# One tile of some groups read from on-chip features instead of gathered from DRAM, in a graph layer on one core

## The chip, the core and the metric

The kernel runs on one core of a Trainium2 chip. The engines of that core are TensorE (PE in the profile, with its weight loads as PEld), VectorE (DVE), ScalarE (ACT), GpSimd (POOL) and SyncE (SP). The metric is the device time of one execution in microseconds; the time given for a kernel is the median of several executions.

## The reference, cut to what matters

There are 12500 nodes with 64 features and 212500 edges with 32 features each, sorted by their destination `col`. Everything is float32.

```python
msg_in = concat([nodes[row], nodes[col], edge_features])       # 64 + 64 + 32 columns
messages = relu(msg_in @ mW1 + mb1) @ mW2 + mb2
aggregated = segment_sum(messages, col, num_segments=12500)
upd = relu(concat([nodes, aggregated]) @ uW1 + ub1) @ uW2 + ub2
out = layernorm(nodes + upd)
```

Two facts of the algebra matter. `nodes[col] @ mW1[64:128]` has only as many different rows as there are different destinations. And `mW2` may be applied after the sum, so that only `relu(...)` and a count per node have to be summed per edge.

## The kernel before

**Groups and tiles.** Edges are taken in groups of 384, three tiles of 128, and there are 554 groups (`G`), the last one not full. As edges are sorted by destination, a group touches at most 32 neighbouring destinations (`W`), its window.

**What one group needs.** `gather(g)` issues one indirect DMA for each of the three tiles: 128 rows of 64 features of `x`, one for each edge's source, from DRAM into `own.s[g % 20]`, by GpSimd (line L132). `onehot(g)` writes beside them, on VectorE (L306), a 128 x 32 one-hot block that tells the edge's place in the window. `turn(g)` transposes each tile of 96 columns on TensorE (L318), and ScalarE copies the result, 96 x 384, into `own.st` and sums the one-hots on the way into `own.counts` (L326). `hidden(g)` multiplies it with a weight tile `own.wm` of 128 rows on TensorE (L339); the 128 rows are 32 rows of the window's own products (made by `windows`, L292, and copied by VectorE, L297), 64 rows of `mW1` for the source's features and 32 rows for the edge's, which SyncE loads beside the transposed tile (L266). ScalarE applies the relu (L349). `sums(g)` multiplies with the one-hots on TensorE (L365), and VectorE adds the result to `agg` and the counts to a row of `xc` (L374, L375) at an address taken from a register.

**Node features on the chip.** `xc` holds all node features transposed, 64 partitions by 12500 columns, with a row of counts in front and a row of ones behind. `places` reads from it with a register address (L285) what `windows` needs, after a load of four registers (L278); that is done once for four groups.

**Order.** The order on every engine is that of the program text; nothing reorders it. Step k runs `turn(k)`, `hidden(k - 2)` and `sums(k - 4)` as one block on TensorE, and then ScalarE's and VectorE's follow-up work. Only the last matmul of a step signals. The blocks alternate between two PSUM sets (`own.ps`), so a step may start only when the follow-up of the step two before is done. Before each step VectorE makes the one-hots of the next one; after it GpSimd gets `gather(k + 16)`.

**Rings.** `own.s` has 20 slots, so the gathers of a group wait for ScalarE's copy of the group 20 before (`copy_by[g - RING]`); `own.h` has 3 slots, `own.st` 3 blocks of four groups, `own.wm` 8. In the last 10 groups the parts are separate steps, and no gather is left to issue. Chunks of 512 finished nodes are updated, normalised and stored in between (`step_update`).

Of the kernel before, what the change touches and what calls it, by code (L numbers as in the profile page):

```python
# [12 lines left out]
I32 = mybir.dt.int32  # L13
AF = mybir.ActivationFunctionType
ALU = mybir.AluOpType
ET = mybir.EngineType
# [3 lines left out]
P = 128  # L20
N = 12500
E = 212500
D = 64
# [5 lines left out]
W = 32  # L29
TG = 3  # L30
GE = TG * P
G = (E + GE - 1) // GE
SB = 4
# [9 lines left out]
BITS = 16  # L43
NEAR_GROUPS = 24
SHORT = 10
TIMES = 4


def tiles_of(g):

    n = min(GE, E - g * GE)
    return [min(P, n - j * P) for j in range((n + P - 1) // P)]
# [23 lines left out]
class Own:  # L76
# [4 lines left out]
    def __init__(self, nc, ctx):  # L81
        def on(name, *shape, of=nc.sbuf_tensor):
            return ctx.enter_context(of(name, list(shape), F32)).ap()

        self.s = [on(f"own_s{i}", P, TG, W + D) for i in range(RING)]
        self.st = [on(f"own_st{i}", P, SB * GE) for i in range(BLOCKS)]
        self.wm = [on(f"own_wm{i}", P, H) for i in range(NW)]
        self.h = [on(f"own_h{i}", P, TG, H) for i in range(NH)]
        self.ident = on("own_ident", P, P)
        self.counts = on("own_counts", D + W, G)  # L90

        self.ps = [on(f"own_ps{i}", P, 3, 512, of=nc.psum_tensor) for i in range(2)]
# [3 lines left out]
def ordered(ctx: ExitStack, tc: tile.TileContext, a, own, ok):  # L96
# [10 lines left out]
    temp = early.enter_context(tc.tile_pool(name="temp", bufs=1))  # L107
    ident, wm, counts = own.ident, own.wm, own.counts


    src_sb = const.tile([P, NT], I32, name="src_sb")
    first = AHEAD * TG
    nc.sync.dma_start(src_sb[:, :first], a["src"][:, :first])

    loads, places_by, copy_by, relu_by, sums_by, wm_by, turn_by = ({} for _ in range(7))
    efs_by, hidden_by = {}, {}

    def after(first, *others):

        tc.declare_no_dep(first.ins, group="quiet", reason="waits for the last of a step")  # L120
        for i in others:
            tc.add_manual_dep(
                first.ins, i.ins.name,
                mybir.DependencyInfo(mybir.DependencyClass.Sync, mybir.DependencyReason.DATA),
                reason="the kernel's own rings",
            )
        return first

    def gather(g):
        s = own.s[g % RING]  # L130
        loads[g] = [
            nc.gpsimd.indirect_dma_start(  # L132
                out=s[:p, j, W:], out_offset=None, in_=x[:, :],
                in_offset=bass.IndirectOffsetOnAxis(
                    ap=src_sb[:p, g * TG + j : g * TG + j + 1], axis=0),
            )
            for j, p in enumerate(tiles_of(g))
        ]
        for i in loads[g]:
            after(i, *([copy_by[g - RING]] if g >= RING else []))  # L140
# [7 lines left out]
    for g in range(AHEAD):  # L148
# [6 lines left out]
    zero = const.tile([P, NP // P], F32, name="zero")  # L155
    nc.vector.memset(zero, 0.0)
    nc.vector.tensor_copy(ident, ident_t)
    iota = iop.tile([P, W], F32, name="iota")
    nc.vector.tensor_copy(iota, iota_i)

# [4 lines left out]
    nc.sync.dma_start(first_i, a["firsts"].to_broadcast([P, G]))  # L165
    dlc_i = temp.tile([P, G * TG], I32, name="dlc_i")
    nc.sync.dma_start(dlc_i, a["dst_cols"])
    nc.sync.dma_start(xc[0:1, :].rearrange("o (p n) -> o p n", p=P), zero)
    nc.sync.dma_start(xc[D + 1 :, :].rearrange("o (p n) -> o p n", p=P), ones[:, : NP // P])
    w1b = const.tile([D + 2, H], F32, name="w1b")  # L170
    nc.vector.memset(w1b[0:1, :], 0.0)
    nc.scalar.dma_start(w1b[1 : D + 1, :], a["mW1"][D : 2 * D, :])
    nc.scalar.dma_start(w1b[D + 1 :, :], a["mb1"][None, :])
    nc.scalar.dma_start(xc[1 : D + 1, :NEAR_NODES], a["xT"][:, :NEAR_NODES])

    wm_loads = [
        [nc.sync.dma_start(t[W : W + D, :], a["mW1"][:D, :]),
         nc.sync.dma_start(t[D + W :, :], a["mW1"][2 * D :, :])] for t in wm
    ]

    def bit(k):

        nodes = [NEAR_NODES + (N - NEAR_NODES) * i // BITS for i in (k, k + 1)]
        tiles = [first + (NT - first) * i // BITS for i in (k, k + 1)]
        nc.sync.dma_start(src_sb[:, slice(*tiles)], a["src"][:, slice(*tiles)])
        nc.sync.dma_start(xc[1 : D + 1, slice(*nodes)], a["xT"][:, slice(*nodes)])


    first_f = own.ps[0].rearrange("p a b -> p (a b)")[:, :G]
# [22 lines left out]
    u1s = const.tile([D, H], F32, name="u1s")  # L212
    nc.scalar.dma_start(u1s, a["uW1"][D:, :])
    ux = const.tile([D + 1, H], F32, name="ux")
    nc.scalar.dma_start(ux[1 : D + 1, :], a["uW1"][:D, :])
# [11 lines left out]
    nc.vector.tensor_copy(ux[0:1, :], wps[0:1, 1])  # L227

# [59 lines left out]
    def windows(b, wp, own_bank=True):  # L288


        xw, n = xws.pop(b)
        did = nc.tensor.matmul(wp[: n * W, :], xw[:, :n, :], w1b, start=True, stop=True)  # L292

        def copies():
            for i in range(n):
                g = b * SB + i
                c = nc.vector.tensor_copy(wm[g % NW][:W, :], wp[i * W : (i + 1) * W, :])  # L297
                after(c, *([did] if own_bank else []), *([hidden_by[g - NW]] if g >= NW else []))
                wm_by[g] = c

        return did, copies

    def onehot(g):
        if g >= G:
            return
        places_by[g] = nc.vector.tensor_tensor(  # L306
            own.s[g % RING][:, :, :W], iota.unsqueeze(1).to_broadcast([P, TG, W]),
            dlc[:, g * TG : (g + 1) * TG].unsqueeze(2).to_broadcast([P, TG, W]), ALU.is_equal,
        )
        after(places_by[g], *([sums_by[g - RING]] if g >= RING else []))  # L310

    def turn(g, ps):


        s = own.s[g % RING]
        xt = ps[: D + W, 0, :GE]
        did = [
            nc.tensor.transpose(xt[:, j * P : j * P + p], s[:p, j, :], ident[:p, :p])  # L318
            for j, p in enumerate(tiles_of(g))
        ]  # L320

        def copy(step):
            t, c, n = columns(g)
            turn_by[g] = step
            copy_by[g] = after(
                nc.scalar.activation(t[: D + W, c : c + n], xt[:, :n], AF.Copy,  # L326
                                     accum_out=counts[:, g : g + 1]), step)
            if g >= BLOCKS * SB:
                after(copy_by[g], hidden_by[g - BLOCKS * SB])
            return [copy_by[g]]  # L330

        return did, [*loads.pop(g), places_by[g]], copy

    def hidden(g, ps):
        t, c, n = columns(g)
        sizes = tiles_of(g)
        pre = ps[:, 1, : TG * H].rearrange("p (j h) -> p j h", h=H)
        did = [
            nc.tensor.matmul(pre[:p, j, :], t[:, c + j * P : c + j * P + p], wm[g % NW],  # L339
                             start=True, stop=True)  # L340
            for j, p in enumerate(sizes)
        ]
        needs = [copy_by[g], wm_by[g], efs_by[g // SB], *(wm_loads[g] if g < NW else ())]
# [12 lines left out]

        return did, needs, relu

    def sums(g, ps):
        h, s = own.h[g % NH], own.s[g % RING]  # L360
        sizes = tiles_of(g)
        sg = ps[:, 2, : (TIMES + 1) * W].rearrange("p (t w) -> p t w", w=W)
        did = [nc.tensor.transpose(sg[0:1, TIMES, :], counts[:W, g : g + 1], ident[:W, :W])]  # L363
        for j, p in enumerate(sizes):
            did.append(nc.tensor.matmul(  # L365
                sg[:, :TIMES, :], h[:p, j, :],
                s[:p, j, :W].unsqueeze(1).to_broadcast([p, TIMES, W]),
                start=j == 0, stop=j == len(sizes) - 1))

        def add(step):  # L370
            sums_by[g] = step
            at = bass.ds(starts.pop(g), W)
            return [
                after(nc.vector.tensor_tensor(agg[:, at], sg[:, 0, :], agg[:, at], ALU.add), step),  # L374
                after(nc.vector.tensor_tensor(xc[0:1, at], sg[0:1, TIMES, :], xc[0:1, at],  # L375
                                              ALU.add), step),
            ]

        return did, [*relu_by[g], copy_by[g]], add
# [99 lines left out]
    for k in range(G):  # L479
# [21 lines left out]
                    made += 1  # L501
        if k + AHEAD < G:
            gather(k + AHEAD)
    while summed < G:
        step((sums, summed))
        summed += 1
# [329 lines left out]
```

## Time and profile before

| | |
|---|---|
| median of 10 runs | 2601.94 us (2600.3 to 2604.2) |
| the profiled execution | 2602.16 us, of which the span is 2600.4 us |
| PE, PEld busy | 1633.2 us (63%), 1425.7 us (55%) |
| POOL busy | 1569.7 us (60%) |
| DVE, ACT busy | 571.9 us (22%), 537.8 us (21%) |
| granted TensorE clock | 0.785 of full speed |
| gathers (L132) | 1661, 945 ns each |
| mean DMA rate | 37 GB/s |

No engine is busy for the whole span, so the shares alone do not name a bound. In the profile, an engine's idle time is put down to what ended it last; "issue" means that no wait is seen, and "remote" that the releaser is not known. Start and length of GpSimd's instructions are rough. The ends of matmuls are modelled.

### The profile page before, as it was taken

What the parts mean: (1) busy time and instruction counts of PE and PEld (TensorE: products, weight loads), DVE (VectorE), ACT (ScalarE), POOL (GpSimd) and SP (SyncE); (2) the same over time, 40 slices, a digit from 0 to 9 for tenths busy, and PEclk for the clock granted to TensorE, in tenths of its full rate; (3) what the DMA queues carried; (4) which work ended last, traced back from release to release, by engine and by line L of the source; (5) the groups of instructions that cost most, each with busy time, mean ns of one, the idle gap of its engine ahead of it and who ended that gap; (6) DMA issues with size and microseconds to landing.
All of it is one profiled execution on the core that took longest, in us unless ns stands there. A gap on an engine that the chain in (4) does not pass through costs nothing.

```text
span 2600.4 us, 30668 instructions
## 1 busy us (share of the span) xinstructions
PE 1633.2 (63%) x9441; PEld 1425.7 (55%) x9441; DVE 571.9 (22%) x3191; ACT 537.8 (21%) x1715; POOL 1569.7 (60%) x1668
## 2 busy tenths in 40 slices
PE   1356666666666666766666666756566666666677
PEld 0355555555555555655555555655555555655565
DVE  4012122221222221212212212212122122221222
ACT  0122122212222221212221222122122222222222
POOL 7566665666666666666666666666666666666650
PEclk9678777787787787778787877777787778777878
DMA  3211111111111111111111111111111111111110
GB/s 89 51 41 39 34 36 35 34 36 36 36 35 37 34 39 31 39 34 36 39 33 37 35 34 38 36 32 38 36 33 38 31 39 33 37 38 34 36 35 13
DMA packets 73364, 96.05 MB, mean 37 GB/s; under 512 B 33451, under 2 KB 40842, under 8 KB 73194
## 3 DMA queue, kind: packets, MB, share of 16 engines
q0 software_dynamic: 53152, 54.51, 12.0%
q1 hardware_dynamic: 19128, 39.03, 5.4%
q8 instruction: 80, 1.31, 0.2%
q14 instruction: 90, 0.74, 0.1%
q10 hardware_dynamic: 914, 0.46, 0.1%
HBM read 90.58 MB, written 3.20 MB: 36 GB/s over the span
## 4 chain that ended last, share of the span: by engine, by line
another core or an unknown queue 41%; PE 29%; issue 16%; ACT 11%; DVE 2%; DMA 0%; DVEq 0%; ACTq 0%
PE own_ps L365 10%; PE own_ps L339 8%; ACT own_h L349 5%; PE own_ps L318 5%; ACT own_st L326 5%; PE u_ps L405 2%; PE own_ps L363 1%; PE u_ps L392 1%; PE u_ps L393 1%; PE own_ps L292 1%; DVE own_wm L297 1%; ACT u L395 0%; DVE xc L375 0%; DMA u1s<-in_uW 0%
## 5 line engine op out<-in xcount | busy, mean ns | idle before, releaser
L132 POOL DMA_INDIRECT own_s<-in_x,src_sb x1661 | 1568.9, 945 | 956.6 <-issue 494.0
L318 PE MATMUL own_ps<-own_ident,own_s 128*96 128x128 f32 x1661 | 366.6, 343 | 832.1 <-ACT own_st L326 426.0
L318 PEld LDWEIGHTS own_ps<-own_ident,own_s 128*96 128x96 f32 x1661 | 234.0, 160 | 897.1 <-ACT own_st L326 443.6
L326 ACT ACTIVATE own_st<-own_ps 96x384 f32<-96x384 f32 x554 | 268.3, 484 | 1896.7 <-remote 1121.1
L365 PE MATMUL own_ps<-own_s,own_h 128*128 128x128 f32 x3322 | 633.1, 337 | 3.5 <-issue 3.5
L339 PE MATMUL own_ps<-own_wm,own_st 128*128 128x128 f32 x3322 | 612.9, 336 | 1.2 <-DVE own_wm L297 1.2
L339 PEld LDWEIGHTS own_ps<-own_wm,own_st 128*128 128x128 f32 x3322 | 570.9, 253 | 4.9 <-DVE own_wm L297 1.6
L365 PEld LDWEIGHTS own_ps<-own_s,own_h 128*128 128x128 f32 x3322 | 513.4, 231 | 29.4 <-issue 2.5
L374 DVE TENSOR_TENSOR agg<-own_ps,agg 128x32 f32 x554 | 106.1, 191 | 1870.4 <-ACT own_h L349 1352.1
L349 ACT ACTIVATE own_h<-own_ps 128x384 f32<-128x384 f32 x553 | 264.2, 478 | 17.2 <-PE own_ps L339 13.2
L297 DVE COPY own_wm<-own_ps 32x128 f32<-32x128 f32 x550 | 155.0, 282 | 7.0 <-issue 1.0
L306 DVE TENSOR_TENSOR own_s<-iota,dlc 128x96 f32<-128x96 f32 x554 | 132.9, 240 | 4.1
L363 PE MATMUL own_ps<-own_ident,own_counts 32*1 32x32 f32 x554 | 106.6, 192 | 4.0 <-ACT own_st L326 1.9
L326 ACT ACTIVATION_READ_ACCUMULATOR own_st<-own_ps 96x1 f32 x554 | 107.2, 194 | 0.0
L375 DVE TENSOR_TENSOR xc<-own_ps,xc 1x32 f32 x554 | 99.0, 179 | 19.8 <-PE u_ps L393 11.5
L363 PEld LDWEIGHTS own_ps<-own_ident,own_counts 32*1 32x1 f32 x554 | 41.1, 74 | 93.5 <-issue 46.3
L405 PE MATMUL u_ps<-u,u 128*128 128x64 f32 (+1 forms) x196 | 49.6, 404 | 29.9 <-ACT u L395 29.9
L405 PEld LDWEIGHTS u_ps<-u,u 128*128 128x128 f32 (+1 forms) x196 | 47.1, 324 | 32.5 <-ACT u L395 32.3
L392 PE MATMUL u_ps<-agg,wc 128*128 128x512 f32 (+1 forms) x50 | 35.5, 800 | 45.7 <-DVE agg L374 36.1
L285 DVE COPY xw<-xc 66x32 f32 x554 | 60.3, 170 | 2.9 <-DMA xc<-in_xT 2.3
L292 PE MATMUL own_ps<-w1b,xw 66*128 66x128 f32 (+1 forms) x276 | 59.0, 298 | 0.0
L292 PEld LDWEIGHTS own_ps<-w1b,xw 66*128 66x128 f32 (+1 forms) x276 | 48.0, 217 | 0.1
(58 smaller groups left out, 203.0 us busy)
## 6 DMA issues: line engine op xcount, KB each, us to landing
own_s<-in_x,src_sb POOLq DMA_INDIRECT x1661
own_st<-in_efT SPq DMA_DIRECT2D x138, 192.0 KB
xin<-in_x SPq DMA_DIRECT2D x24, 128.0 KB
out<-o SPq DMA_DIRECT2D x24, 128.0 KB
xc<-in_xT SPq DMA_DIRECT2D x12, 179.2 KB
dlc_i<-in_dst_cols SPq DMA_DIRECT2D x1, 831.0 KB
xc<-in_xT SPq DMA_DIRECT2D x4, 179.5 KB
src_sb<-in_src SPq DMA_DIRECT2D x13, 50.5 KB
```

Of the source, the lines that this page charges most:

```text
L132: nc.gpsimd.indirect_dma_start(out=s[:p, j, W:], out_offset=None, in_=x[:, :], in_offset=bass.IndirectOffsetOnAxis(ap=src_sb[:p, g * TG + ...
L292: did = nc.tensor.matmul(wp[: n * W, :], xw[:, :n, :], w1b, start=True, stop=True)
L297: c = nc.vector.tensor_copy(wm[g % NW][:W, :], wp[i * W : (i + 1) * W, :])
L306: places_by[g] = nc.vector.tensor_tensor(own.s[g % RING][:, :, :W], iota.unsqueeze(1).to_broadcast([P, TG, W]), dlc[:, g * TG : (g + 1) * ...
L318: nc.tensor.transpose(xt[:, j * P : j * P + p], s[:p, j, :], ident[:p, :p])
L326: nc.scalar.activation(t[: D + W, c : c + n], xt[:, :n], AF.Copy, accum_out=counts[:, g : g + 1]), step)
L339: nc.tensor.matmul(pre[:p, j, :], t[:, c + j * P : c + j * P + p], wm[g % NW], start=True, stop=True)
L349: relu_by[g] = [nc.scalar.activation(h, pre, AF.Relu)]
L363: did = [nc.tensor.transpose(sg[0:1, TIMES, :], counts[:W, g : g + 1], ident[:W, :W])]
L365: did.append(nc.tensor.matmul(sg[:, :TIMES, :], h[:p, j, :], s[:p, j, :W].unsqueeze(1).to_broadcast([p, TIMES, W]), start=j == 0, stop=j = ...
L374: after(nc.vector.tensor_tensor(agg[:, at], sg[:, 0, :], agg[:, at], ALU.add), step),
L405: nc.tensor.matmul(o_ps[:p, k], u[:, k:q:n], u2, start=True, stop=True)
```

## The change

From group 44 on, the last tile of every 16th group (31 tiles) and, from group 48 on, that of every 24th (21 tiles) is no longer gathered. Its 128 source columns are copied from `xc`, one instruction for each edge with a column address from a register, into a 128 x 128 tile `own.f` whose lower 64 rows are zero: by VectorE for the first kind, by ScalarE for the second. The copies of a tile are spread over the 16 or 24 steps that end 4 steps before the group's own, 8 a step on VectorE, 5 or 6 on ScalarE, behind the follow-up work of the step; eight registers are loaded ahead of each eight copies. For such a group, ScalarE's copy of the transposed tiles is made in two instructions (features of two tiles, one-hots of three), and TensorE multiplies the third tile in two matmuls, one for the copied columns and one for window and edge rows.

So that a copied column and the weight rows meet at the same partitions, features come first in every layout: in `own.s`, `own.wm`, `xc` and `w1b`. The counts are transposed from partitions 64 to 95 of `own.counts`. Four tiles of 128 columns are zeroed at the start, and one more small DMA loads the copied tiles' source numbers (`cols_sb`, 52 x 128).

```diff
+ONE = TG - 1
+BY_DVE = range(44, G - 16, 16)
+BY_ACT = range(48, G - 16, 24)
+COPIED = {**dict.fromkeys(BY_DVE, (ET.DVE, BY_DVE)), **dict.fromkeys(BY_ACT, (ET.Activation, BY_ACT))}
+SLACK = 3
+REGS = 8
...
-        self.s = [on(f"own_s{i}", P, TG, W + D) for i in range(RING)]
+        self.s = [on(f"own_s{i}", P, TG, D + W) for i in range(RING)]
...
-            for j, p in enumerate(tiles_of(g))
+            for j, p in enumerate(tiles_of(g)) if not copied(g, j)
...
+    for t in [t for pair in own.f.values() for t in pair]:
+        nc.vector.memset(t[D:, :], 0.0)
...
+    cols_sb = const.tile([len(COPIED), P], I32, name="cols_sb")
+    nc.sync.dma_start(cols_sb, a["src_rows"])
...
+    def source_columns(g):
+        _, way = COPIED[g]
+        return own.f[way][way.index(g) % 2]
+
+    def copies_of(k):
+
+        for n, (g, (engine, way)) in enumerate(COPIED.items()):
+            at = k - (g - SLACK - way.step)
+            if not 0 <= at < way.step:
+                continue
+            f, used, ahead = source_columns(g), g - 2 * way.step, held[engine]
+            for r in range(at * P // way.step, (at + 1) * P // way.step):
+                if r % REGS == 0:
+                    _, ahead[:] = nc.values_load_multi_w_load_instructions(
+                        cols_sb[n : n + 1, r : r + REGS], engines=[engine], min_val=0,
+                        max_val=N - 1,
...
+                    )
+                column = f[:D, r : r + 1], xc[:D, bass.ds(ahead[r % REGS], 1)]
+                c = (nc.vector.tensor_copy(*column) if engine == ET.DVE
+                     else nc.scalar.activation(*column, AF.Copy))
+                after(c, *([hidden_by[used]] if used in way else []))
+                columns_by[g] = [c]
...
+            parts = [(slice(0, D + W), n)]
+            if g in COPIED:
+                parts = [(slice(0, D), n - P), (slice(D, D + W), n)]
+            for to, m in parts:
+                copy_by[g] = after(
+                    nc.scalar.activation(
+                        t[to, c : c + m], xt[to, :m], AF.Copy,
+                        **({"accum_out": counts[to, g : g + 1]} if to.stop > D else {})), step)
...
+        for j, p in enumerate(sizes):
+            cols = t[:, c + j * P : c + j * P + p]
+            parts = [(cols, w)]
+            if copied(g, j):
+                parts = [(source_columns(g), w), (cols[D:, :], w[D:, :])]
+            for i, (edges, weights) in enumerate(parts):
+                did.append(nc.tensor.matmul(pre[:p, j, :], edges, weights, start=i == 0,
+                                            stop=i == len(parts) - 1))
...
         if k + AHEAD < G:
             gather(k + AHEAD)
+        copies_of(k)
```

More of the change, by code (lines that the diff above doesn't have):

```diff
@@ L88, in __init__ @@
         self.h = [on(f"own_h{i}", P, TG, H) for i in range(NH)]
+        self.f = {way: [on(f"own_f{len(way)}_{i}", P, P) for i in range(2)]
+                  for way in (BY_DVE, BY_ACT)}
         self.ident = on("own_ident", P, P)
@@ L108, in ordered, with copied @@
     ident, wm, counts = own.ident, own.wm, own.counts
+    def copied(g, j):
+        return g in COPIED and j == ONE
     src_sb = const.tile([P, NT], I32, name="src_sb")
@@ L115, in ordered @@
     loads, places_by, copy_by, relu_by, sums_by, wm_by, turn_by = ({} for _ in range(7))
-    efs_by, hidden_by = {}, {}
+    efs_by, hidden_by, columns_by = {}, {}, {}
+    held = {ET.DVE: [], ET.Activation: []}
     def after(first, *others):
@@ L132, in gather @@
             nc.gpsimd.indirect_dma_start(
-                out=s[:p, j, W:], out_offset=None, in_=x[:, :],
+                out=s[:p, j, :D], out_offset=None, in_=x[:, :],
                 in_offset=bass.IndirectOffsetOnAxis(
@@ L167, in ordered @@
     nc.sync.dma_start(dlc_i, a["dst_cols"])
-    nc.sync.dma_start(xc[0:1, :].rearrange("o (p n) -> o p n", p=P), zero)
+    nc.sync.dma_start(xc[D : D + 1, :].rearrange("o (p n) -> o p n", p=P), zero)
     nc.sync.dma_start(xc[D + 1 :, :].rearrange("o (p n) -> o p n", p=P), ones[:, : NP // P])
     w1b = const.tile([D + 2, H], F32, name="w1b")
-    nc.vector.memset(w1b[0:1, :], 0.0)
-    nc.scalar.dma_start(w1b[1 : D + 1, :], a["mW1"][D : 2 * D, :])
+    nc.vector.memset(w1b[D : D + 1, :], 0.0)
+    nc.scalar.dma_start(w1b[:D, :], a["mW1"][D : 2 * D, :])
     nc.scalar.dma_start(w1b[D + 1 :, :], a["mb1"][None, :])
-    nc.scalar.dma_start(xc[1 : D + 1, :NEAR_NODES], a["xT"][:, :NEAR_NODES])
+    nc.scalar.dma_start(xc[:D, :NEAR_NODES], a["xT"][:, :NEAR_NODES])
     wm_loads = [
-        [nc.sync.dma_start(t[W : W + D, :], a["mW1"][:D, :]),
+        [nc.sync.dma_start(t[:D, :], a["mW1"][:D, :]),
          nc.sync.dma_start(t[D + W :, :], a["mW1"][2 * D :, :])] for t in wm
@@ L185, in bit @@
         nc.sync.dma_start(src_sb[:, slice(*tiles)], a["src"][:, slice(*tiles)])
-        nc.sync.dma_start(xc[1 : D + 1, slice(*nodes)], a["xT"][:, slice(*nodes)])
+        nc.sync.dma_start(xc[:D, slice(*nodes)], a["xT"][:, slice(*nodes)])
+    cols_sb = const.tile([len(COPIED), P], I32, name="cols_sb")
+    nc.sync.dma_start(cols_sb, a["src_rows"])
     first_f = own.ps[0].rearrange("p a b -> p (a b)")[:, :G]
@@ L214, in ordered @@
     ux = const.tile([D + 1, H], F32, name="ux")
-    nc.scalar.dma_start(ux[1 : D + 1, :], a["uW1"][:D, :])
+    nc.scalar.dma_start(ux[:D, :], a["uW1"][:D, :])
     ub1 = const.tile([H, 1], F32, name="ub1")
@@ L226, in ordered @@
     nc.vector.tensor_copy(wc, wps[:, 0])
-    nc.vector.tensor_copy(ux[0:1, :], wps[0:1, 1])
+    nc.vector.tensor_copy(ux[D : D + 1, :], wps[0:1, 1])
     off = temp.tile([P, G * TG], F32, name="off")
@@ L296, in copies @@
                 g = b * SB + i
-                c = nc.vector.tensor_copy(wm[g % NW][:W, :], wp[i * W : (i + 1) * W, :])
+                c = nc.vector.tensor_copy(wm[g % NW][D : D + W, :], wp[i * W : (i + 1) * W, :])
                 after(c, *([did] if own_bank else []), *([hidden_by[g - NW]] if g >= NW else []))
@@ L306, in onehot @@
         places_by[g] = nc.vector.tensor_tensor(
-            own.s[g % RING][:, :, :W], iota.unsqueeze(1).to_broadcast([P, TG, W]),
+            own.s[g % RING][:, :, D:], iota.unsqueeze(1).to_broadcast([P, TG, W]),
             dlc[:, g * TG : (g + 1) * TG].unsqueeze(2).to_broadcast([P, TG, W]), ALU.is_equal,
@@ L310, in onehot @@
         after(places_by[g], *([sums_by[g - RING]] if g >= RING else []))
+    def source_columns(g):
[12 more added lines that the diff above has]
+                        max_val=N - 1,
+                        skip_runtime_bounds_check_because="a source is one of the nodes",
+                    )
[4 more added lines that the diff above has]
+                columns_by[g] = [c]
     def turn(g, ps):
@@ L324, in copy @@
             turn_by[g] = step
[L325 to L329, printed above, removed]
+            parts = [(slice(0, D + W), n)]
[6 more added lines that the diff above has]
+                        **({"accum_out": counts[to, g : g + 1]} if to.stop > D else {})), step)
+                if g >= BLOCKS * SB:
+                    after(copy_by[g], hidden_by[g - BLOCKS * SB])
             return [copy_by[g]]
@@ L337, in hidden @@
         pre = ps[:, 1, : TG * H].rearrange("p (j h) -> p j h", h=H)
[L338 to L343, printed above, removed]
+        did, w = [], wm[g % NW]
+        for j, p in enumerate(sizes):
[6 more added lines that the diff above has]
+                                            stop=i == len(parts) - 1))
+        needs = [copy_by[g], wm_by[g], efs_by[g // SB], *(wm_loads[g] if g < NW else ()),
+                 *columns_by.pop(g, [])]
         def relu(step):
@@ L361, in sums @@
         sizes = tiles_of(g)
-        sg = ps[:, 2, : (TIMES + 1) * W].rearrange("p (t w) -> p t w", w=W)
-        did = [nc.tensor.transpose(sg[0:1, TIMES, :], counts[:W, g : g + 1], ident[:W, :W])]
+        sg = ps[:, 2, : TIMES * W].rearrange("p (t w) -> p t w", w=W)
+        lo = D if sizes[-1] == P else 0
+        line = ps[0:1, 2, TIMES * W :][:, : D + W - lo]
+        did = [nc.tensor.transpose(line, counts[lo:, g : g + 1], ident[lo : D + W, lo : D + W])]
+        line = line[:, D - lo :]
         for j, p in enumerate(sizes):
             did.append(nc.tensor.matmul(
-                sg[:, :TIMES, :], h[:p, j, :],
-                s[:p, j, :W].unsqueeze(1).to_broadcast([p, TIMES, W]),
+                sg, h[:p, j, :],
+                s[:p, j, D:].unsqueeze(1).to_broadcast([p, TIMES, W]),
                 start=j == 0, stop=j == len(sizes) - 1))
@@ L374, in add @@
                 after(nc.vector.tensor_tensor(agg[:, at], sg[:, 0, :], agg[:, at], ALU.add), step),
-                after(nc.vector.tensor_tensor(xc[0:1, at], sg[0:1, TIMES, :], xc[0:1, at],
-                                              ALU.add), step),
+                after(nc.vector.tensor_tensor(xc[D : D + 1, at], line,
+                                              xc[D : D + 1, at], ALU.add), step),
             ]
@@ L817 @@
         "src": padded(v["src"], NT * P, 0).reshape(NT, P).T,
+        "src_rows": padded(v["src"], NT * P, 0).reshape(NT, P)[
+            [g * TG + ONE for g in COPIED]],
         "dst_cols": padded(v["dst"], G * TG * P, -1).reshape(G * TG, P).T,
```

## The prediction

> **What bounds the kernel now.** I read the page's engine groups first, then the list of waits, then the timelines of single engines, and last a table by stretches. Page and waits first: line, engine, operation, tiles, count; busy time and mean ns; idle time before and what ended it; for waits total, times, longest.
>
> ```profile
> L132 POOL DMA_INDIRECT own_s<-in_x,src_sb x1661 | 1568.9, 945 | 956.6 <-issue 494.0
> ...
> L326 ACT ACTIVATE own_st<-own_ps 96x384 f32<-96x384 f32 x554 | 268.3, 484 | 1896.7 <-remote 1121.1
> ```
>
> ```profile
> ACT own_st L326 <- remote: 1121.1, 179, 22.8
> POOL own_s L132 <- issue: 494.0, 1480, 3.0
> POOL own_s L132 <- ACT own_st L326: 451.2, 165, 9.9
> ```
>
> GpSimd's line is full of gathers and of two kinds of gaps: 0.30 us after each one, and 165 waits of 2.73 us on ScalarE's copy. 1568.9 + 956.6 = 2525.5 us, and the last gather starts at 2526.2. The wait is the 20-slot ring: counted in the trace, the gathers are 19 to 20 groups ahead of the copies from group 20 to 530. So data are never late, and by this list alone GpSimd waits for the steps and not they for it. The timelines say more. GpSimd, then ScalarE, in one stretch (start, length, idle before):
>
> ```profile
> 980.02 0.94 POOL L132 DMA_INDIRECT own_s<-in_x,src_sb  x1 [2.12 <-ACT own_st L326]
> 981.27 0.94 POOL L132 DMA_INDIRECT own_s<-in_x,src_sb  x1 [0.30 <-issue]
> ...
> 990.00 0.94 POOL L132 DMA_INDIRECT own_s<-in_x,src_sb  x1 [0.30 <-issue]
> 993.73 0.94 POOL L132 DMA_INDIRECT own_s<-in_x,src_sb  x1 [2.78 <-ACT own_st L326]
> ```
>
> ```profile
> 983.85 0.49 ACT L326 ACTIVATE own_st<-own_ps 96x384 f32<-96x384 f32 x1 [2.87 <-DVE own_s L306]
> ...
> 992.89 0.49 ACT L326 ACTIVATE own_st<-own_ps 96x384 f32<-96x384 f32 x1 [8.09 <-remote]
> ...
> 993.74 0.48 ACT L326 ACTIVATE own_st<-own_ps 96x384 f32<-96x384 f32 x1
> ```
>
> A burst is nine gathers 1.25 us apart (980.02 to 990.00), then a pause of 3.73 us. One copy comes early (983.85), the next only at 992.89, 2.89 us after the burst's last gather, and the third right behind it. Yet TensorE's matmuls for that copy ended at 986.43. They seem to signal only once the burst has run out. This holds whatever the burst's length: over all bursts the late copy comes 2.4 us (6 gathers, 14 bursts), 2.9 us (9, 136 bursts) and 2.4 to 3.3 us (12 and 15, 18 bursts) after the last gather, but 8.7, 12.9, 17.3 and 21.7 us after the first. Last, the stretch where gathers run and the one after the last of them:
>
> ```profile
> 1200.00:2400.00 1200.00, 777.60 (x4454) 679.56 (x4454) 257.15 (x1480) 251.58 (x808) 742.44 (x787) 0.78 0.17 36
> 2529.00:2543.00 14.00, 12.81 (x106) 11.68 (x104) 4.47 (x27) 5.72 (x18) 0.00 (x0) 1.00 0.05 15
> ```
>
> ```profile
> 2529.63 0.49 ACT L326 ACTIVATE own_st<-own_ps 96x384 f32<-96x384 f32 x1 [1.35 <-PE own_ps L365]
> ...
> 2531.83 0.49 ACT L326 ACTIVATE own_st<-own_ps 96x384 f32<-96x384 f32 x1 [1.25 <-PE own_ps L292]
> ```
>
> In the first, 262 groups take 1200 us, 4.58 us each. In the second (POOL 0.00) a step takes 2.2 us. The same steps run at half the time once no gathers run beside them. I conclude that the gather stream paces the kernel though its data are early: a cycle is 9 x 1.25 us plus (2.89 + 0.84 - 1.25) = 2.48 us, 13.7 us for three groups, 4.57 each.
>
> **The change, part by part.**
>
> *Gathers removed.* 31 + 21 = 52, each 0.945 + 0.30 = 1.25 us of a burst: 52 x 1.25 = -65 us. A burst of three groups is then eight gathers; the pause stays. If the steps and not the stream set the cycle, this is 0.
>
> *VectorE's copies.* In 31 x 16 = 496 steps there are eight copies of 64x1 and one load of eight registers. The nearest rows are those of `places`:
>
> ```profile
> 1019.39 1.17 DVE L297 COPY own_wm<-own_ps 32x128 f32<-32x128 f32 x4
> ...
> 1020.49 0.41 DVE L285 COPY xw<-xc 66x32 f32 x4
> ```
>
> Four register-addressed copies take 0.41 us, so eight take 0.8. The load before them took 0.34 us (L278, median of 139) and is hidden under the 1.17 us here; behind the two additions (L374, L375, 0.3 us) it will show in part. Bounds for the step are 0.8 and 1.2 us; I take 1.2, as the load has little over it. VectorE's 22% share hides the sum, 496 x 1.2 = 595 us, but not its place: the copies stand in front of the next one-hot (0.24 us), and that step on TensorE waits for it. What stands behind them is the one-hot, the next additions and, through these, the first step of each burst. It starts 1.5 us after the late copy now, and would start 1.2 us later. The trace has that case: after L297 and L285 (1.6 us more) the first step starts 2.3 us and not 0.7 us after the burst's first gather. The 33 bursts of that kind take 4.61 us a group, the 107 others 4.55. So 0.06 us for each of 497 groups: +30 us; lower bound 0, upper bound 165 bursts x 1.2 = +198 us, if none of it is covered. What covers it is the stretch between the steps' recorded end and the signal (986.43 to 992.89 above).
>
> *ScalarE's copies.* 16/3 of 64x1 a step and a load of eight registers in two steps of three. Nearest rows: READ_ACCUMULATOR 194 ns, a 128x4 ACTIVATE 297 ns (L414); 1.0 to 1.6 us a step, and up to 0.23 us for loads. Behind them waits the second copy of a pair (993.74), whose place in the ring is wanted 3.75 us later, and its relu, which the second step of a burst needs when the first ends, some 4 us later: nothing, with at most 1.6 us a burst, 165 x 1.6 = +264 us, if that cover goes.
>
> *Split copy of 52 groups.* One more ACTIVATE, 0.39 us apart in the timeline. It counts where GpSimd waits for that very copy, one group in three: 17 x 0.37 = +6 us; bounds 0 and 19.
>
> *Small parts.* Two more passes of a matmul in 52 steps, 2 x 0.11 to 2 x 0.21 us: 11 to 22 us of TensorE, in the same cover: 0. Four memsets and a DMA of 26 KB before the first step: under 1 us, taken as 0. Moving features to the front changes addresses and no count: 0. No wait is added to a copied column but that of its group's hidden step, for work done 6 steps earlier.
>
> *Two rules that speak against it.* A gather with four VectorE copies inside it is no longer than others: 135 gathers overlap L285, mean 945 ns, the rest 945; the sum takes 0 for it. The Trainium skill's "DMA: Bandwidth & Descriptors" (section "SWDGE vs HWDGE vs iDMA") says that GpSimd writes descriptors to SBUF state from which VectorE locks it out while in a 2-port mode; if each of 3968 copies held a gather for its whole 0.1 us, that would be +397 us. The trace disagrees with any such size. The register load took 342 ns in the trace. The same page (section "Latency and other measured facts") puts such a load at some 600 ns at least; that would be 0.26 us more a step and, at 0.06 us a group for 1.6 us, 5 us more.
>
> Sum: -65 + 30 + 6 = -29 us from the profiled execution's 2602.2 us: 2573 us. The profiled execution is 0.2 us above the median, so nothing is added for that.
>
> **The rivals.**
>
> *All of the gain stays.* VectorE's 1.2 us vanishes in the cover: -65 + 6 gives 2543 us. For it: 6 us of cover in most bursts. Against: the 4.55 and 4.61 above.
>
> *The steps set the cycle, and it gets slower.* GpSimd is 19 to 20 groups ahead, so taking away gathers gives 0, and VectorE's 1.2 us lies in the way of the first step of all 165 bursts: 2602 + 198 = 2800 us. It decides where the late copy follows the steps' chain and not the last gather, that is where it comes well over 2.9 us after that gather. For it: the full ring, and two of three steps each wait for ScalarE and VectorE. Against: the distance to the last gather is the same for bursts of 6, 9, 12 and 15. A part of it, with half the bursts bound so, gives 2602 - 32 + 99 = 2669.
>
> *A draw.* The first steps of two bursts in five come so late that these shrink to two groups (4.76 us a group in the 14 that exist, 0.21 above 4.55): 199 x 0.21 = +42, and 298 x 0.06 = +18 for the rest: 2602 - 65 + 42 + 18 + 6 = 2603 us.
>
> **How the numbers follow.** The measurement can tell about 0.2% (5 us) from no change. The forecast has 0.52 (its own range 2550 to 2597), the whole gain 0.22, the draw 0.07, of which 0.04 is within 0.2% and 0.03 slower, and steps that set the cycle, in part or whole, 0.19. So faster 0.74, same 0.04, slower 0.22. The range starts at 2532, below the full 65 us by a few, and reaches to 2650, into the partly step-bound case; above it are 0.15, below it 0.03.
>
> **What would show it.** Right: L132 has 1609 gathers of 945 ns at 1.25 us, 160 to 170 waits on ScalarE's copy of 2.7 us, and a late copy 2.9 us after a burst's last gather, also in bursts of eight; VectorE's new group is near 100 ns a copy. Wrong: a longer distance between the last gather and the copy, gathers longer than 945 ns, more bursts of two groups, or a copy's price several times that of L285. If the last gather starts at 2461 + 36 = 2497 us, the sum is right; if it starts at 2526 or later, the pacing was read wrongly.

## The result, and the profile after

The changed kernel takes 2688.14 us (median of 8 runs, 2680.8 to 2693.0), the kernel before 2601.61 us (28 runs): a ratio of 1.0331 [1.0322, 1.034], 86.5 us slower. The forecast was 2573 us and faster. The time is outside the range.

One fact has to be known before any other number is read: chips differ here. The kernel before takes 2602 us on the chip of this comparison and 2603 us on one of the six chips of the experiments (perhaps the same one), but 2103 to 2106 us on the five others. In what follows "a 2602 chip" and "a 2103 chip" stand for these two kinds, and kernels are compared with the kernel before on the same chip.

The page of the changed kernel (columns as in the prediction), and its list of waits:

```profile
L145 POOL DMA_INDIRECT own_s<-in_x,src_sb x1609 | 1518.5, 944 | 1092.3 <-ACT own_st L372 673.4
...
L349 DVE COPY own_f<-xc 64x1 f32 x3968 | 428.9, 144 | 213.4 <-issue 208.6
```

```profile
POOL own_s L145 <- ACT own_st L372: 673.4, 272, 8.2
POOL own_s L145 <- issue: 409.7, 1322, 1.9
```

The 52 gathers are gone, each still 944 ns, and the time in them fell by 50.4 us. But GpSimd now waits 272 times for ScalarE's copy and not 165 times, 673.4 us and not 451.2. Its idle time before gathers grew from 956.6 to 1092.3 us: 136 us more idle and 50 us less in gathers are, together, the 86 us of the result. The last gather starts at 2611.4 us. The timeline of GpSimd shows the new pattern (start, length, idle before):

```profile
1009.47 0.94 POOL L145 DMA_INDIRECT own_s<-in_x,src_sb  x1 [2.50 <-ACT own_st L372]
...
1014.45 0.94 POOL L145 DMA_INDIRECT own_s<-in_x,src_sb  x1 [0.30 <-issue]
1018.06 0.94 POOL L145 DMA_INDIRECT own_s<-in_x,src_sb  x1 [2.66 <-ACT own_st L372]
...
1024.30 0.94 POOL L145 DMA_INDIRECT own_s<-in_x,src_sb  x1 [0.30 <-issue]
1027.64 0.94 POOL L145 DMA_INDIRECT own_s<-in_x,src_sb  x1 [2.40 <-ACT own_st L372]
```

Bursts are five or six gathers, two groups, and no longer nine: counted in the trace, 191 of 275 bursts have six and 50 five, where 150 of 190 had nine. Each still ends in a pause of 3.3 us from gather to gather. So there are 85 pauses more. VectorE and TensorE in one of these bursts show what comes late:

```profile
1018.42 0.18 DVE L432 TENSOR_TENSOR xc<-own_ps,xc 1x32 f32 x1
1019.16 0.96 DVE L349 COPY own_f<-xc 64x1 f32 x8 [0.56 <-issue]
1020.05 0.24 DVE L324 TENSOR_TENSOR own_s<-iota,dlc 128x96 f32<-128x96 f32 x1
```

```profile
1020.39 0.51 PE L360 MATMUL own_ps<-own_ident,own_s 128*96 128x128 f32 x3 [0.62 <-issue]
```

The additions end at 1018.60. Then VectorE stands idle for 0.56 us while it loads eight registers, copies for 0.89 us, and only at 1020.05 makes the next step's one-hot. This ends at 1020.29, and the step's first transpose starts 0.1 us later. TensorE was idle for 0.62 us before it. The one-hot stands 1.45 us later than it did, and TensorE waits for it. Over all bursts the first step starts 2.67 us (median) after the burst's first gather; it was 0.72 us. From the copy of group 20 to that of group 530 a group takes 4.748 us and not 4.572: 510 x 0.176 = 90 us, the whole difference. The setup and the end took the same in both kernels, to 1.2 us.

### The profile page after: what moved, and what is told of

Its sections match the earlier page's. It is cut to its first block, busy times and chain, and to the rows that moved or that the text cites. A ratio compares the mean times of both kernels' runs of the same rounds, so it can differ in the third digit from the quotient of the medians.

```text
span 2688.6 us, 45023 instructions
## 1 busy us (share of the span) xinstructions
PE 1689.2 (63%) x9545; PEld 1457.6 (54%) x9545; DVE 1061.1 (39%) x7163; ACT 827.7 (31%) x4455; POOL 1519.3 (57%) x1616
## 4 chain that ended last, share of the span: by engine, by line
PE 49%; issue 17%; another core or an unknown queue 15%; ACT 10%; ACTq 3%; DVE 2%; DVEq 0%
PE own_ps L422 19%; PE own_ps L392 15%; PE own_ps L360 9%; ACT own_f L350 3%; ACT own_h L401 3%; ACT own_st L372 3%; PE own_ps L419 2%; ACTq L343 2%; PE u_ps L462 2%; PE u_ps L449 1%; ACTq L350 1%; PE u_ps L450 1%; PE own_ps L310 1%; DVE agg L431 1%
## 5 line engine op out<-in xcount | busy, mean ns | idle before, releaser
L145 POOL DMA_INDIRECT own_s<-in_x,src_sb x1609 | 1518.5, 944 | 1092.3 <-ACT own_st L372 673.4
L372 ACT ACTIVATE own_st<-own_ps 96x384 f32<-96x384 f32 (+2 forms) x606 | 286.2, 472 | 1698.0 <-PE own_ps L422 1061.1
L422 PE MATMUL own_ps<-own_s,own_h 128*128 128x128 f32 x3322 | 643.9, 341 | 1.2 <-issue 1.2
L392 PE MATMUL own_ps<-own_wm,own_st 128*128 128x128 f32 (+1 forms) x3322 | 632.7, 339 | 1.4 <-DVE own_wm L315 1.4
L392 PEld LDWEIGHTS own_ps<-own_wm,own_st 128*128 128x128 f32 (+1 forms) x3322 | 574.4, 252 | 16.4 <-issue 11.4
L422 PEld LDWEIGHTS own_ps<-own_s,own_h 128*128 128x128 f32 x3322 | 522.0, 234 | 28.1 <-issue 0.8
L349 DVE COPY own_f<-xc 64x1 f32 x3968 | 428.9, 144 | 213.4 <-issue 208.6
L350 ACT ACTIVATE own_f<-xc 64x1 f32 x2688 | 304.4, 193 | 9.0 <-issue 6.2
L372 ACT ACTIVATION_READ_ACCUMULATOR own_st<-own_ps 96x1 f32 (+1 forms) x554 | 106.4, 192 | 0.6
L303 DVE COPY xw<-xc 66x32 f32 x554 | 80.3, 213 | 50.2 <-issue 49.2
```

Source lines behind the costliest of these rows:

```text
L145: nc.gpsimd.indirect_dma_start(out=s[:p, j, :D], out_offset=None, in_=x[:, :], in_offset=bass.IndirectOffsetOnAxis(ap=src_sb[:p, g * TG + ...
L349: c = (nc.vector.tensor_copy(*column) if engine == ET.DVE else nc.scalar.activation(*column, AF.Copy))
L350: else nc.scalar.activation(*column, AF.Copy))
L372: nc.scalar.activation(t[to, c : c + m], xt[to, :m], AF.Copy, **({"accum_out": counts[to, g : g + 1]} if to.stop > D else {})), step)
L392: did.append(nc.tensor.matmul(pre[:p, j, :], edges, weights, start=i == 0, stop=i == len(parts) - 1))
L422: did.append(nc.tensor.matmul(sg, h[:p, j, :], s[:p, j, D:].unsqueeze(1).to_broadcast([p, TIMES, W]), start=j == 0, stop=j == len(sizes) - 1))
```

## Experiments

The theory (A) was that VectorE's copies and loads, standing ahead of the next one-hot, make the first steps of bursts late, and that this shrinks the bursts. Its rivals were that the loss is VectorE's or ScalarE's added work as such, wherever it stands, or that gathers left out are no gain at all.

**First set, on a 2103 chip: each part of the change alone.** The layout alone, either engine's tiles alone, and an order with the one-hot ahead of the copies:

```diff
--- a1_onehot_first
+    onehot(1)
...
-        onehot(k + 1)
...
+        onehot(k + 2)
         copies_of(k)
--- a2_dve_only
+BY_ACT = range(48, 48)
--- a3_act_only
+BY_DVE = range(44, 44)
--- a4_layout_only: both of them empty
```

> The changed kernel with one order altered: each step's one-hot is made one step earlier, ahead of the register copies, so TensorE's next step does not wait for them. Theory 1 (the one-hot behind the copies makes the first step of a burst 1.9 us late, so GpSimd's bursts break off after two groups): bursts of three groups come back, 8 or 9 gathers, and the 52 saved gathers show, 2540 to 2570 us. Theory 2 (the copies' work itself, on VectorE or ScalarE, lengthens the chain of the steps): 2660 us or more. Theory 3 (the moved partitions cost it): 2680 us.

> Only VectorE's 31 tiles are copied; ScalarE copies none. Theory 1: the one-hot is as late as in the changed kernel, 21 fewer gathers are saved (+26 us), some of ScalarE's share goes: 2680 to 2710 us, bursts of two groups. Theory 2 with ScalarE as the cause: 2602 - 39 + 5, about 2565 us, bursts of three.

> Only ScalarE's 21 tiles are copied; VectorE copies none. Theory 1: bursts of three groups, 2602 - 26 + 3, about 2580 us. Theory 2 with ScalarE as the cause: 2660 us or more.

> No tile is copied, all 1661 are gathered; the layouts with the features first stay. Theories 1 and 2: 2602 us within 5. Theory 3: 2680 us.

Against 2102.72 us: layout alone 2100.68, 0.999 [0.998, 1.0]; VectorE's tiles alone 2061.84, 0.9801 [0.9784, 0.9817]; ScalarE's alone 2075.68, 0.9872 [0.9855, 0.9888]; both, one-hot first, 2036.88, 0.9683 [0.9667, 0.9699]. That is 41, 27 and 66 us less, where 1.25 us for each of 31, 21 and 52 gathers make 39, 26 and 65. On this chip the gathers left out are the whole account. The page of the layout alone shows why:

```profile
L144 POOL DMA_INDIRECT own_s<-in_x,src_sb x1661 | 1568.2, 944 | 507.2 <-issue 378.2
```

The gathers are as long as ever, but GpSimd never waits for ScalarE. It is 2 groups ahead of the copies and not 20, and a group takes 3.742 us, three gathers of 1.25 us. Not one of the copies 20 to 529 comes over 0.6 us after the recorded end of its matmuls; on the 2602 chip 345 of 510 do. So here the gathers do set the pace, without any pause, and every one that is left out shows.

**The changed kernel itself on a 2103 chip**, beside the one-hot-first order and VectorE's tiles once more, and a kernel in which the 52 tiles are neither gathered nor copied (no `copies_of(k)`, `own.f` zero).

> The changed kernel as it is, on another chip. Where the kernel before takes some 2600 us, all theories expect 2688 again. Where it takes some 2103 us (a chip on which GpSimd runs only 2 to 3 groups ahead and its gathers set the pace): theory A, 'the late one-hot costs only where TensorE's signals wait for a burst to run out', expects the gathers' full 65 us less, about 2037; theory B, 'the one-hot behind VectorE's copies is late in every copied step whatever the chip', expects 496 steps x 1 to 1.9 us less whatever is covered, 2100 to 2500.

> The changed kernel without the register loads and column copies: the 52 tiles are neither gathered nor copied, their features count as zero. All that is left of the change is 52 gathers fewer and small parts. Where the kernel before takes some 2600 us: the pacing of the prediction (the gather stream sets the cycle) expects 2602 - 65 + 6 = about 2540; a rival (the steps set the cycle, the stream only fits in) expects 2595 to 2610. Where the kernel before takes 2103: 2037 by either.

The changed kernel takes 2037.12 us against 2103.57, 0.9687 [0.967, 0.9703]: here it is 66 us faster. Removal alone gives 2036.16, 0.9681 [0.9664, 0.9697], so the copies cost nothing here. The two repeats gave 2037.15 (one-hot first) and 2063.21 (VectorE's tiles alone). The sign of the change depends on the chip. Theory B of the expectations, a one-hot that costs in every step on every chip, falls.

**Without gathers, on a 2602 chip.** `gather` issues nothing from group 20 on; only the steps remain.

```diff
--- e1_before_free (on the kernel before)
-            for j, p in enumerate(tiles_of(g))
+            for j, p in enumerate(tiles_of(g)) if g < RING
--- e2_after_free: the same in the changed kernel
--- e3_first_free: the same with the one-hot ahead of the copies
```

> The kernel before without the gathers of groups 20 to 553 (their slots keep the features of earlier groups): only the steps are left to set the time. On a chip where the kernel before takes 2103 us, all theories expect steps of 2.15 to 2.3 us: 554 x 2.2 + 90 = 1270 to 1370 us. On a chip where it takes some 2600 us: if the gathers are what holds TensorE's signals there, 1300 to 1450; if something else does, 2300 to 2600.

> The changed kernel, also without the gathers from group 20 on. Theory A (VectorE's copies delay the next one-hot, and this the next step, wherever steps and not gathers set the pace): VectorE's row in a copied step is adds 0.3 + load 0.56 + copies 0.96 + one-hot 0.25 + a quarter of the windows' 1.6, about 2.5 us against steps of 2.2, in one chain with the step: 150 to 500 us more than the kernel before without gathers. Rival (the added work lies beside TensorE's in steps too, and the loss of the changed kernel came from its gathers): less than 30 us more.

> As the run before it, with the one-hot made ahead of the copies, a step earlier. Theory A in its narrow form (it is the place of the one-hot): at most 100 us above the kernel before without gathers. Its wide form (VectorE has too much work for a step, in whatever order): within 50 us of the changed kernel without gathers.

They take 1506.42, 2027.59 and 1591.0 us; the kernel before on that chip takes 2603.18. In the table by stretches, the same 900 us of each (length, busy time of PE, PEld, DVE, ACT and POOL with counts, granted TensorE clock, DMA share, GB/s):

```profile
500.00:1400.00 900.00, 796.01 (x6059) 707.11 (x6058) 345.85 (x2020) 353.33 (x1099) 0.00 (x0) 1.00 0.09 25
```

```profile
500.00:1400.00 900.00, 690.07 (x4411) 597.00 (x4412) 493.81 (x3493) 399.00 (x2180) 0.00 (x0) 0.89 0.07 19
```

```profile
500.00:1400.00 900.00, 785.53 (x5707) 685.12 (x5706) 660.08 (x4526) 515.83 (x2821) 0.00 (x0) 0.98 0.09 24
```

Three things follow. Gathers are what slows the steps on a 2602 chip: in the first run no copy is late (0 of 510), the clock is 1.00, and a group takes 2.53 us. Where steps set the pace, the change costs 521 us. And most of that is the place of the one-hot: in the third run VectorE copies as much (its busy share is even higher) and the cost is 85 us. Only the place of the one-hot differs:

```profile
1000.41 0.18 DVE L432 TENSOR_TENSOR xc<-own_ps,xc 1x32 f32 x1
1001.16 0.95 DVE L349 COPY own_f<-xc 64x1 f32 x8 [0.57 <-issue]
1002.04 0.24 DVE L324 TENSOR_TENSOR own_s<-iota,dlc 128x96 f32<-128x96 f32 x1
```

```profile
1008.06 0.26 DVE L324 TENSOR_TENSOR own_s<-iota,dlc 128x96 f32<-128x96 f32 x1
1008.64 0.96 DVE L349 COPY own_f<-xc 64x1 f32 x8 [0.32 <-issue]
```

In the second run the one-hot ends at 1002.28 and the transposes start at 1002.43; in the third the next step finds its one-hot made.

The 85 us are not the price of the copies alone, for the new order also puts the one-hot ahead of `places`, which stands before it once in four steps in the kernel before, and that kernel was not run in the new order. What this is worth shows in groups 532 to 539, where nothing is copied or gathered any more. The same eight groups in the three runs:

```profile
1426.59:1445.58 19.00, 16.63 (x134) 15.01 (x133) 6.67 (x40) 7.63 (x24) 0.00 (x0) 1.00 0.08 22
```

```profile
1934.47:1954.05 19.58, 16.75 (x134) 15.04 (x133) 7.87 (x40) 7.63 (x24) 0.00 (x0) 1.00 0.07 21
```

```profile
1514.79:1533.44 18.65, 16.75 (x134) 15.04 (x133) 7.67 (x40) 7.63 (x24) 0.00 (x0) 1.00 0.08 22
```

What is left of the change there, the layout (the moved features and the counts' transposition), costs 0.58 us, and the earlier one-hot gains 0.93. Over 554 groups that would be some 40 us of cost and 65 us of gain. By this estimate some 370 of the 436 us between the second run and the third are the place of the one-hot behind the copies, and copies and splits still cost some 85 + 65 - 40 = 110 us with the one-hot first.

**One-hot first, gathers in, on the same 2602 chip.**

> The changed kernel with the one-hot ahead of the copies, all gathers in. Where the kernel before takes some 2600 us: theory A narrow expects 2540 to 2602, wide 2640 to 2690. Where the kernel before takes 2103: 2037 by both, since gathers set the pace there.

2638.23 us against 2603.18, 1.0141 [1.0124, 1.0158]. Beside the changed kernel's 2688 that is 50 us less, so the place of the one-hot, behind copies and `places`, is the larger part of the loss. It is not all: this kernel is still 35 us above the kernel before, though it gathers 52 tiles fewer. Both forms of the theory missed: the narrow one asked for 2602 at most, the wide one began at 2640. Nor did the bursts of three groups come back:

```profile
POOL own_s L145 <- ACT own_st L372: 604.7, 254, 7.8
```

This bears on the mechanism of theory A. One burst of this run, of six gathers, in GpSimd's first gather, TensorE's first step (start and last matmul) and ScalarE's copy for it:

```profile
1005.60 0.95 POOL L145 DMA_INDIRECT own_s<-in_x,src_sb  x1 [2.14 <-ACT own_st L372]
1006.54 0.51 PE L360 MATMUL own_ps<-own_ident,own_s 128*96 128x128 f32 x3 [0.30 <-ACT own_f L350]
1008.53 0.39 PE L310 MATMUL own_ps<-w1b,xw 66*128 66x128 f32 x2
1014.28 0.49 ACT L372 ACTIVATE own_st<-own_ps 96x384 f32<-96x384 f32 x1 [6.60 <-remote]
```

The first step starts 0.94 us after the first gather and ends at 1008.92, and yet its copy starts only at 1014.28. Counted in the traces (groups 20 to 529), 104 bursts of this run have a first step within 1.0 us of their first gather; 78 of them have six gathers, and in 96 the copy of the first step comes over 0.6 us after the recorded end of its matmuls. In the kernel before there are 106 such bursts; 99 have nine gathers, and 1 such copy is late. So the bursts stay short although the first step is early: a late first step is not, or not alone, what shortens them. Why the signals are late in one kernel and not in the other was not found.

**What remains, four cases in stretches.** Two attempts to run removal alone and VectorE's tiles with the one-hot first on a 2602 chip fell on 2103 chips.

> The changed kernel without the register loads and column copies: 52 tiles are neither gathered nor copied, their features count as zero. Where the kernel before takes some 2600 us: the prediction's pacing (the gather stream sets the cycle, a burst of three groups is eight gathers) expects 2602 - 65 + 6 = about 2540; a rival (the steps set the cycle, and gathers fit in) expects 2595 to 2610. Where the kernel before takes 2103: 2037.

> One-hot ahead of the copies, VectorE's 31 tiles only; ScalarE's 21 are gathered again. Where the kernel before takes some 2600 us: if ScalarE's copies and loads between the follow-ups of two steps are what remained of the loss (1.5 us and not 0.85 between the two copies of a pair), 2565 to 2605, that is at least 35 us less than the 2638 with both; if VectorE's load and copies are what remained, 2620 to 2660. Where the kernel before takes 2103: 2062.

They gave 2036.37 us, 0.9679 [0.9662, 0.9695], and 2064.55 us, 0.9809 [0.9793, 0.9826]; the second attempt 2035.77 and 2062.31. That is 1.27 to 1.35 us for each gather, and says nothing of a 2602 chip. So two kernels held all cases one after the other, by lists of copied groups for each stretch (`BY_DVE`, `BY_ACT`, and `LEFT_OUT`, neither gathered nor copied) and a list of steps in which the one-hot goes first; the second kernel also gathers nothing from group 300 on.

> Four stretches of steps in one kernel. 32 to 126: VectorE's tiles alone, one-hot behind the copies; 146 to 258: eleven tiles neither gathered nor copied (their features count as zero); 268 to 384: ScalarE's tiles alone; 395 to 519: VectorE's tiles alone, one-hot ahead of the copies. In the kernel before these take 4.58, 4.57, 4.58 and 4.57 us a group where it takes 2602, and 3.75 each where it takes 2103. Where it takes 2602: the prediction's pacing expects 4.57 - 11 x 1.25 / 112 = 4.45 in the second stretch, the rival (the steps set the cycle, the gathers fit in) 4.55 to 4.60. First stretch: late one-hot 4.68 to 4.80. Third: 4.62 or more if ScalarE's copies are what remained of the loss, 4.52 if they lie beside other work. Fourth: 4.50 to 4.53 in that case, 4.60 or more if VectorE's load remained. Where it takes 2103: 3.67 to 3.73, 3.62, 3.70, 3.67.

> Eight stretches in one kernel; from group 300 on nothing is gathered (features of earlier groups stay in the slots), and ten tiles are neither gathered nor copied. Steps 33 to 81: VectorE's tiles alone, one-hot behind the copies; 88 to 140: tiles left out; 149 to 197: ScalarE's alone; 205 to 253: VectorE's alone, one-hot ahead. Then without gathers: 307 to 355, 363 to 411 and 415 to 463 the first, third and fourth of these, 480 to 516 only the split copy and matmuls. With gathers, where the kernel before takes 2602 (4.53, 4.53, 4.48, 4.56 us a group there): pacing by the gathers 4.41 in the second, steps 4.50 or more; late one-hot 4.65 or more in the first; ScalarE's copies 4.55 or more in the third if they are the rest of the loss. Where it takes 2103: 3.71, 3.62, 3.70, 3.67. Without gathers (kernel before without gathers 2.53, 2.52, 2.57, 2.57; changed kernel 3.56): late one-hot 3.3 to 3.6 in the first; the other three 2.5 to 2.75, and the one of ScalarE and VectorE's that is nearer to 2.75 is what is left of the loss with the one-hot first.

Both fell on 2103 chips as well. The first (2063.33 us) gave 3.707, 3.626, 3.699 and 3.674 us a group, against 3.745, 3.745, 3.733 and 3.745 in the kernel with the layout alone. Tiles left out gain 0.119 us a group, and 11 x 1.25 / 112 = 0.123 was expected. The half of the second kernel (1852.9 us) that has gathers tells no more. The half without is this, by stretches, with the kernel before without gathers (`e1_before_free`, on the 2602 chip) taking 2.53, 2.52, 2.57 and 2.57 us a group over the same steps at a clock of 1.00:

```profile
1139.50:1302.70 163.20, 124.25 (x822) 108.32 (x823) 92.23 (x649) 49.02 (x151) 0.00 (x0) 0.91 0.07 19
1322.60:1449.10 126.50, 109.50 (x820) 96.94 (x820) 53.55 (x270) 71.86 (x401) 0.00 (x0) 0.99 0.08 24
1458.80:1584.20 125.40, 111.27 (x825) 96.64 (x824) 95.25 (x653) 49.70 (x151) 0.00 (x0) 1.00 0.09 25
1627.60:1732.20 104.60, 90.61 (x630) 79.50 (x629) 41.64 (x210) 39.77 (x118) 0.00 (x0) 0.93 0.08 23
```

VectorE's tiles with the one-hot behind take 163.20 / 48 = 3.40 us a group, 0.87 more; ScalarE's 2.64, 0.12 more; VectorE's with the one-hot ahead 2.61, 0.04 more. The last stretch has no copies of columns at all, only five groups with a split copy and split matmuls, and takes 104.60 / 36 = 2.90, that is 0.34 a group or 2.4 us for each such group. That was not expected (2.5 to 2.75). It is not all the split, and it is uneven. Blocks of four there without a copied group take 9.79 us, where `e1_before_free` takes 9.50: that much is the layout. Of the five blocks with a copied group, two take 1.05 us more than this, two take 4.05 us more, and the fifth, in which a finished chunk is updated, no more than other such blocks. In ScalarE's stretch too a block takes 9.79 us beside the copies, so 0.07 of its 0.12 us a group are the layout. Around one of the two longest blocks, TensorE:

```profile
1671.63 0.94 PE L431 MATMUL own_ps<-own_s,own_h 128*128 128x128 f32 x6
1674.62 0.50 PE L369 MATMUL own_ps<-own_ident,own_s 128*96 128x128 f32 x3 [2.05 <-ACT own_h L410]
...
1678.47 0.85 PE L369 MATMUL own_ps<-own_ident,own_s 128*96 128x128 f32 x3
1679.11 1.49 PE L401 MATMUL own_ps<-own_wm,own_st 128*128 128x128 f32 x6
```

The split copy of group 496 takes ScalarE 0.4 us more, in a step whose successor also waits for the windows' copies, since every copied group of this stretch, as of the changed kernel, is the first of its block of four (in the other three stretches none is). TensorE stands still for 2.05 us, and after it runs at a granted clock of half for 6.8 us (from 1675.17 in the clock's record): three transposes take 0.85 and not 0.50 us, six matmuls 1.49 and not 0.83. The only other time at half clock in this stretch, from 1722.95, lies in the other of the two longest blocks.

## Why the prediction was wrong, point by point

**Two steps failed: "A burst of three groups is then eight gathers; the pause stays", and the price of VectorE's copies, "+30 us".** The result lies 115 us above the forecast of 2573. With the one-hot first VectorE's copies no longer stand in its way; -65 + 6 gives 2543 us for such a kernel, and it took 2638. So some 95 of the 115 us are not in the +30, and some 20 are (50 us and not 30). In GpSimd's line 52 gathers went, but the number of pauses did not stay: bursts fell from three groups to two, 275 bursts and not 190, and with 85 pauses more the idle time grew by 136 us. Putting the one-hot first takes 50 us off; the cause of the rest stays open.

**The price of VectorE's copies** was near in what it says of one step: 1.2 us was taken and 1.45 us measured, of which 0.56 us is idle time before the copies. The loads of eight registers (L343) took 608 ns in the median, not the 342 ns of a load of four. The page cited for it, the Trainium skill's "DMA: Bandwidth & Descriptors" (section "Latency and other measured facts"), has some 600 ns, and was nearer than the row that the sum used. The failure is in the cover. 0.06 us a group came from the 33 bursts behind `places`, where one step in four is late; the change makes every step late. The runs showed 50 us for the place of the one-hot alone on a 2602 chip (2688 to 2638), what it gains by standing ahead of `places` included, and 0.87 us a group, layout included, where steps set the pace.

**The draw foresaw the short bursts; its reason for them is not shown.** Bursts did shrink to two groups. The rival put this at two bursts in five; it is nearly all of them, and the group takes 4.748 us, where 4.76 was read from the 14 bursts that existed. The prediction had the right row and gave the case 0.07. Its reason was that first steps come late. They do in the changed kernel (2.67 us, median), but with the one-hot first 78 of 104 bursts with an early first step are as short.

**The reading of what paces the kernel was half right.** That gathers slow the steps on this chip is shown: 4.57 us a group with them, 2.53 without, and the late signals go with them. That each gather removed gives 1.25 us is shown for 2103 chips, where there is no pause, and not for 2602 chips. By its own test the pacing was misread: the last gather starts at 2611 and not near 2497, and bursts of two groups are many. Its other sign did not come: the late copy is 2.45 us after a burst's last gather, no longer than before and as the prediction read it for bursts of six (2.4). So a cycle can still be added up as it was there, 6 x 1.25 + (3.3 - 1.25) = 9.55 us for two groups, 4.78 each; what it had wrong is how many groups a cycle holds. The rival in which the steps set the cycle "in part" (2669 us) is nearest by its number, but its sign, a late copy well over 2.9 us after the last gather, is not seen.

**The split copy, "+6 us" and "Small parts" of 0, were undersized where steps set the pace.** With the one-hot first and no gathers, the blocks of four with a copied group take 1.39 us (standard error 0.13) more than in the kernel before without gathers, the others 0.27 (0.05). So 52 x (1.39 - 0.27) = 58 us lie where the split is, about half of the 110 that copies and splits cost there. The prediction priced one ACTIVATE and looked only at GpSimd behind it; VectorE's windows and the next step stand behind it too, and TensorE's clock behind these. On the 2602 chip with gathers the same split gives 0.57 (0.48) and 0.04 (0.41), which can't be told apart.

**ScalarE's copies were over-priced and rightly hidden**: 193 ns each but 0.56 us for five, where 1.0 to 1.6 us were allowed, and at most 0.12 us a group where steps set the pace. VectorE's copies do not lengthen gathers: the 787 gathers that overlap one take 944 ns and the 822 others as much, so the 0 for the rule on GpSimd's descriptors was right. Setup cost nothing, as said. The layout cost nothing on a 2103 chip; where steps set the pace it costs 0.07 us a group (19.58 and not 19.00 us for eight), so "changes addresses and no count: 0" does not hold everywhere. On a 2602 chip with gathers it was not run alone.

**What stays open** is the 35 us of the one-hot-first kernel on a 2602 chip. Either the 52 gathers are worth nothing there and the split copies make the 35, or they are worth their 65 us and some 100 us of other work is uncovered. The layout, up to 40 us where steps set the pace, may be part of it. Removal alone and the layout alone would tell; neither ran on a 2602 chip. The layout ran once, on a 2103 chip. Removal alone ran five times, inside other kernels or by itself.

No version that ran on both kinds of chip beats both kernels on both; VectorE's tiles alone with the one-hot first ran only on 2103 chips. With the one-hot first the change is as good as the changed kernel where that is faster (0.9685 [0.9669, 0.9701]) and loses 1.4% and not 3.3% where it is slower.

## What to carry to other kernels

On an engine that works in the order of the program text, the price of added work is not only its length but what is queued behind it in the same step: put what another engine waits for first, and the filler after it. A small effect read from the rare case must not be multiplied over all steps, since the cover that makes it small may be used up by the second late step. And before work is taken from one stream and given to another, find out which of the two sets the pace, on more than one chip: here the answer, and with it the sign of the change, differed between chips. Last, when an order is changed as a control, look at everything that the moved instruction passes: here it passed `places` as well as the copies.

## What the runs showed of the hardware

The same kernel took 2602 us on one or two chips and 2103 to 2106 us on five. On the first kind, TensorE's signals come up to 10 us after the recorded end of its matmuls while indirect gathers run, and on time without gathers; its clock is at half for 1122 of the 2542 us in the clock's record with them (the kernel before) and for 17 of 1409 without (`e1_before_free`). On a 2103 chip the layout alone, with all its gathers, has it at half for 228 of 2054 us. Without gathers the two kinds agree: the eight plain groups above take 19.58 us in `e2_after_free` on a 2602 chip and 19.57 in `i1_two_halves` on a 2103 chip. As the ends of matmuls are modelled, the profile can't tell a late signal from matmuls that end later. Why chips differ in this was not found.

A pause of TensorE of 2.05 us, by its recorded ends, was followed by 6.8 us at half clock. The Trainium skill's "TensorE: Matmul & The Clock Gate" (section "What's actually happening") has the clock fall after at least one idle window of some 3.4 us; the stretches of half clock here are multiples of 3.41 us, as its window is, but the recorded idle time before this one is shorter. In the second run without gathers the clock is 0.89, and TensorE spends 690 us on 4411 matmuls, 156 ns each; in the first it is 796 us on 6059, 131 ns each. So some of the 521 us there may be slower matmuls, beside the wait for the one-hot.
